# A seventh buffer for the scan's state tiles, with one buffer less in three other rings

## The chip, the cores and the metric

The kernel runs on one core of one Trainium2 chip. The metric is the device time of one execution in microseconds (us), as the median of several runs. A profile of one further execution is shown beside it. Engines are named as in the profile: PE is TensorE (PEld its weight loads), DVE is VectorE, ACT is ScalarE, POOL is GpSimd, SP is SyncE, which issues nearly all DMAs here; an engine's name with a q is its queue.

## The reference, cut to what matters

Two layers of a "metaformer" over an image batch `x` of 4 images of 64 x 64 positions and 128 channels. Layer 0 mixes with a four-direction state-space scan and then applies a soft mixture of 64 experts; layer 1 mixes rows and columns and then applies spectral filters (an FFT convolution). The change is in the scan of layer 0:

```python
x0 = xc.reshape(Bsz, DI, L)                       # DI = 256 channels, L = 4096 positions
x1 = jnp.transpose(xc, (0, 1, 3, 2)).reshape(Bsz, DI, L)
xs = jnp.stack([x0, x1, x0[..., ::-1], x1[..., ::-1]], axis=1)      # K = 4 directions
...
def step(h, xs):                                  # over L, per image, direction, channel, N = 16 states
    ut, dt, bt, ct = xs
    dA = jnp.exp(dt[..., None] * A)
    h = dA * h + (dt * ut)[..., None] * bt[:, :, None, :]
    y = jnp.einsum('bkdn,bkn->bkd', h, ct)
    return (h, y)
```

After it come the sum over the directions, a layer norm, a gate `z`, an output projection and the residual. All is float32.

## The kernel before, in words

**Scan part.** For each of 4 images and 4 directions the 4096 positions are cut into 8 chunks of 512. A chunk has 16 steps, one for each state index n; so there are 4 x 4 x 8 x 16 = 2048 steps s. Channels lie on partitions, in two halves of 128, and a step handles [128, 2, 512]:

- SP loads `bc` (L1460 to L1464): row n of B and of C for this chunk, spread over all partitions. Six buffers, asked for five steps ahead.
- ACT makes `da` = exp(delta x A_n), two activations (L1471). Five buffers, asked for three steps ahead.
- DVE makes `db` = (delta x u) times B into PSUM (L1501; the factor is `dx` in SBUF at n = 0 and its PSUM copy `du`, made by ACT at L1452, at the others), then runs two hardware scans h = da h + db along the 512 positions into `hh` (L1507).
- POOL keeps the last column for the next chunk (`hst`, L1516) and multiplies `hh` in place by C (L1517).
- PE transposes `hh` in eight 128 x 128 matmuls into the PSUM tile `y` (L1543), which adds up over the 16 steps. There is one `y`; at a chunk's end ACT copies it to `ys` (L1411, `put_away`), and only then may the next chunk's first transpose start.

`hh` is a ring of six tiles (L1497), 4 KiB per partition each. Scan s writes the tile that step s-6 used, so it waits until PE's transposes of step s-6 are done. The loop is skewed: its pass s traces scan s, POOL's work of s-1 and PE's of s-2. The next chunk's delta, `dl` and `dx` are made during the present chunk (`step_sizes`, L1342 to L1405: PE projection, ACT functions, POOL differences, PE sum).

**Side work.** All other stages are generators that yield weights. `deal` (L1420) runs after the first and after the second half of each step's transposes and takes as many pieces as are due, so that each image's share is used up evenly. What it traces is tied behind the step's instructions on each engine (`add_manual_dep`, "queued behind"), and later transposes on PE behind the side work. Within these ties the order of each engine's queue is laid down when the kernel is built, by readiness in the builder's own picture of time; so on ACT, for instance, a `da` that is traced later can stand ahead of a copy that is traced earlier. On the chip each queue keeps that order. During image 0 the side work is the front stages of the other images; during image b > 0 it is `after_scans`, `experts_and_sums`, `to_slots` of image b-1 and part of the spectral filters (`convolve`).

**Tail.** After the last scan the same stages for image 3 run (`first_stages`), woven with the remaining filters, then the return to positions (`from_slots`). The scan's tiles are gone then.

**The other rings.** `after_scans` works in 16 groups of 256 positions, as a pipeline whose later stages are traced first in each pass: load, `add` (evicts `y`, L534, ring of eight), norm sums, refine, a pause, `apply` (loads the gate `z`, L541 and L542, ring of five), a pause, `turn` (transposes of `y`, L552), the POOL product with `z` (L591), a pause, projection, store. `y` here is an SBUF tile of 2 KiB, apart from the scan's PSUM `y`; `z` is 2 KiB. `experts_and_sums` reads the first expert weights in 32 pairs through `w1t` tiles of 4 KiB (pool `ex1`, L822, ring of eight; loads at L835, asked for three pairs ahead; matmuls at L842). These stages run beside the scan and again in the tail.

Of the kernel before, what the change touches and what calls it, by code (L numbers as in the profile page):

```python
# [10 lines left out]
F32 = mybir.dt.float32  # L11
# [6 lines left out]
P = 128  # L18
B, H, W, C = 4, 64, 64, 128
L = H * W  # L20
DI, N, K, R = 256, 16, 4, 8
# [7 lines left out]
SC = 512  # L29
# [49 lines left out]
def kernel(  # L79
# [153 lines left out]
    def bank(shape, name):  # L233

        if side["ones"]:
            settle(1)
            return side["ones"].tile(shape, F32, name=name, tag="ps")
        n = int(np.prod(shape[1:]))
        ap = pair(name)[0 : shape[0], 0, 0:n]
        if len(shape) == 2:  # L240
            return ap
        sizes = {f"d{i}": d for i, d in enumerate(shape[1:])}
        names = " ".join(sizes)
        return ap.rearrange(f"p ({names}) -> p {names}", **sizes)
# [263 lines left out]
    def after_scans(b):  # L508

        with tc.tile_pool(name="po", bufs=2) as po:  # L510
            yk, y, z, xr, st, yT, pr = {}, {}, {}, {}, {}, {}, {}

            def rows(g):
                return slice(256 * g, 256 * (g + 1))

            def load(g):
                for k in range(K):
                    t = po.tile([P, 2, DI], F32, name=f"yk{k}")
                    yk[g, k] = t
                    if k % 2 == 0:  # L520
                        src = y_d[b][k, rows(g), :].rearrange("(q p) d -> p q d", p=P)
                        nc.sync.dma_start(t, src)
                    else:
                        byc = y_d[b][k].rearrange("(w q i) d -> i w q d", w=W, i=2)
                        for i in range(2):
                            nc.sync.dma_start(
                                t[i * W : (i + 1) * W], byc[i][:, 2 * g : 2 * g + 2]
                            )

            def add(g):  # L530
                ps = bank([P, 2, DI], "yk_ps")
                for k in range(K):
                    nc.tensor.matmul(ps, ident, yk.pop((g, k)), start=(k == 0), stop=(k == K - 1))  # L533
                y[g] = po.tile([P, 2, DI], F32, name="y", bufs=8)  # L534
                evict_soon(lambda: evict(y[g], ps))

            def sums(g):
                st[g] = norm_sums(po, y[g], 2, DI, eps5)

            def apply(g):  # L540
                z[g] = po.tile([P, 2, 256], F32, name="z", bufs=5)  # L541
                nc.sync.dma_start(z[g], z_d[b][:, :, rows(g)].rearrange("h p l -> p h l"))  # L542
                xr[g] = po.tile([P, 2, C], F32, name="xr", bufs=7)
                nc.sync.dma_start(xr[g], x[b, rows(g), :].rearrange("(q p) c -> p q c", p=P))
                norm_apply(y[g], y[g], st[g], 2)

            def turn(g):
                yT[g] = po.tile([P, 2, 256], F32, name="yT", bufs=4)
                ps = bank([P, 2, 2, P], "yt_ps")
                for h in range(2):  # L550
                    for q in range(2):
                        nc.tensor.transpose(  # L552
                            ps[:, h, q, :], y[g][:, q, h * P : (h + 1) * P], ident
                        )
                for h in range(2):
                    nc.scalar.activation(
                        yT[g][:, h, :],
                        ps[:, h].rearrange("p q t -> p (q t)"),
                        AF.Identity,
                        bias=nb[:, h : h + 1],  # L560
                        scale=nw[:, h : h + 1],
                    )

            def project(g):

                ps = bank([P, 2, C], "pr_ps")
                nc.tensor.matmul(ps, ident, xr[g], start=True, stop=False, skip_group_check=True)
                for q in range(2):
                    for h in range(2):
                        nc.tensor.matmul(  # L570
                            ps[:, q, :],
                            yT[g][:, h, q * P : (q + 1) * P],
                            w_out_t[:, h, :],
                            start=False,
                            stop=(q == 1 and h == 1),
                            skip_group_check=True,
                        )
                pr[g] = po.tile([P, 2, C], F32, name="pr", bufs=4)
                evict_soon(lambda: evict(pr[g], ps))

            yield from pipelined(
                16,
                (1.0, load),
                (2.2, add),
                (2.0, sums),
                (1.2, lambda g: norm_refine(po, st[g], 2, DI, 1e-5)),
                None,
                (1.2, apply),
                None,
                (1.0, turn),  # L590
                (1.2, lambda g: nc.gpsimd.tensor_mul(yT[g], yT[g], z[g])),  # L591
                None,
                (1.4, project),
                (
                    0.4,
                    lambda g: nc.sync.dma_start(
                        x1_d[b][rows(g), :].rearrange("(q p) c -> p q c", p=P), pr[g]
                    ),
                ),
            )  # L600
# [114 lines left out]
    def experts_and_sums(b):  # L715

        with tc.tile_pool(name="mk", bufs=1) as kp:
# [3 lines left out]
            with tc.tile_pool(name="ga", bufs=2) as gp:  # L721
# [70 lines left out]
                po = bank([P, E], "po_ps")  # L792
# [26 lines left out]

            EG = 2  # L820
            hT = kp.tile([P, HC, E], F32, name="hT")
            with tc.tile_pool(name="ex1", bufs=8) as ep:  # L822
                mask = ep.tile([P, 2, 32 * 32], F32, name="mask1", bufs=1)
                nc.gpsimd.memset(mask, 0.0)
                yield 2.0
                nc.gpsimd.tensor_copy(
                    mask[:, :, 0 : 32 * 32 : 33], pooled.rearrange("p (g e) -> p g e", g=2)
                )
                b1t = ep.tile([E, HID], F32, name="b1t", bufs=1)
                nc.sync.dma_start(b1t, w1[:, C, :])  # L830
                w1t = {}

                def load1(i):
                    w1t[i] = ep.tile([P, EG, HID], F32, name="w1t")
                    nc.sync.dma_start(  # L835
                        w1t[i], w1[i * EG : (i + 1) * EG, 0:C, :].rearrange("e d h -> d e h")
                    )

                def first(i):
                    for e in range(EG):  # L840
                        g, r = divmod(i * EG + e, 32)
                        nc.tensor.matmul(  # L842
                            hps[32 * g : 32 * g + 32, :],
                            mask[:, g, 32 * r : 32 * r + 32],
                            w1t[i][:, e, :],
                            start=(r == 0),
                            stop=(r == 31),
                            skip_group_check=True,
                        )

                for i in range(3):
                    load1(i)
                yield LAG
                hps = bank([E, HID], "h1_ps")
                for i in range(E // EG):
                    if i + 3 < E // EG:
                        load1(i + 3)
                    first(i)
                    yield 4.5
                h1 = ep.tile([E, HID], F32, name="h1", bufs=1)  # L860
                evict(h1, hps)
                yield LAG
                nc.gpsimd.tensor_add(h1, h1, b1t)
                yield LAG
                gelu = nc.scalar.activation(h1, h1, AF.Gelu)
                with tc.issue_after(gelu.ins):
                    nc.scalar.preload_act_table_set("natural_log_exp_and_others")
                yield LAG
                ps = bank([P, HC, E], "hT_ps")
                for q in range(HC):  # L870
                    nc.tensor.transpose(ps[:, q, :], h1[:, q : HID : HC], ident[0:E, 0:E])
                evict(hT, ps)
                yield LAG
            with tc.tile_pool(name="ex2", bufs=6) as ep:
# [31 lines left out]
                for i in range(E // EG):  # L906
                    if i * EG % 32 == 0:
                        g = i * EG // 32
# [421 lines left out]
    with ExitStack() as c0:  # L1330
        pb = c0.enter_context(tc.tile_pool(name="pb", bufs=2))
# [112 lines left out]
        bcs, das, hhs, dus, hsts, ys = {}, {}, {}, {}, {}, {}  # L1444
# [9 lines left out]
        for s in range(-5, total + 2):  # L1454
# [23 lines left out]
            if 0 <= s < total:  # L1478
# [12 lines left out]
                if i + 1 < len(chunks):  # L1491
# [2 lines left out]
                        sizes[i + 1] = step_sizes(nb_, nk, nci)  # L1494
                    if n >= 1:
                        next(sizes[i + 1][3], None)
                hhs[s] = pb.tile([P, 2, SC], F32, name="hh", bufs=6)  # L1497
                db = bps.tile([P, 2, SC], F32, name="db")

                src = sizes[i][1] if n == 0 else dus[i]  # L1500
# [25 lines left out]
            if n == 0:  # L1526
                y = ys[c] = bps.tile([P, 4, 2, P], F32, name="y")
# [165 lines left out]
```

## Time and profile before

| | |
|---|---|
| median of 3 runs | 10992.57 us (10983.71 to 10992.90) |
| the profiled execution | 10988.03 us, its span 10986.2 us |
| scan part, first `db` to the last step | 277 to 8797 us |
| tail | 8797 us to the end |
| busy, share of the span | PE 79%, DVE 75%, POOL 62%, ACT 57% |
| PE clock granted, scan part / tail | 0.83 / 0.99 |
| DMA | 1980 MB, 180 GB/s over the span |

A row of the costliest groups reads: line, engine, operation, written tile <- read tiles, shapes, count | busy us, mean ns of one | idle us of the engine just before them, and what ended most of it. In the slices each digit is the busy share of one fortieth of the span (275 us) in tenths. In the timeline the columns are start, duration, engine, line, operation and, in brackets, the idle time ahead of it with what ended it.

### The profile page before, as it was taken

How to read it: one execution, taken by the hardware profiler on the slowest of the kernel's cores; microseconds unless marked ns; L12 is line 12 of the kernel's file. 1: busy time of each engine (PE TensorE's matmuls, PEld its weight loads, DVE VectorE, ACT ScalarE, POOL GpSimd, SP SyncE). 2: the span in 40 equal slices, each digit the busy share in tenths (PEclk: the TensorE clock that was granted, in tenths of full speed). 3: DMA queues.
4: the chain of work that ended last, by engine and by line, in shares of the span. 5: the costliest groups of instructions: out<-in, count | busy, mean ns of one | idle time of the engine just before them, and what ended most of it. 6: DMA issues, size and time to landing. Idle time of an engine off the chain costs nothing. (4 is left out here: it accounts for less than half of the span.)

```text
span 10986.2 us, 119383 instructions
## 1 busy us (share of the span) xinstructions
PE 8713.2 (79%) x35936; PEld 4918.8 (45%) x35936; DVE 8219.8 (75%) x7094; ACT 6229.3 (57%) x12156; POOL 6822.5 (62%) x6102
## 2 busy tenths in 40 slices
PE   6787777657876777768777677687777799999999
PEld 2444444434454444455543344455344444355443
DVE  0898989987998999989989899798799922222322
ACT  4767676758576655675755557657556534134221
POOL 1777777977777888877777788677688811001000
PEclk9798888768888888878878888798788999999999
DMA  2465656657656666657566567475666564544554
GB/s 95 165 203 173 208 180 214 207 185 219 229 191 196 196 189 194 210 166 264 174 187 179 173 189 225 163 258 161 197 189 195 180 163 122 149 126 105 136 135 118
DMA packets 901464, 1980.28 MB, mean 180 GB/s; under 512 B 101562, under 2 KB 415578, under 8 KB 899290
## 3 DMA queue, kind: packets, MB, share of 16 engines
q1 hardware_dynamic: 900826, 1972.65, 58.8%
q8 instruction: 293, 4.80, 0.2%
q14 instruction: 345, 2.83, 0.1%
HBM read 1766.77 MB, written 205.52 MB: 180 GB/s over the span
## 5 line engine op out<-in xcount | busy, mean ns | idle before, releaser
L1517 POOL TENSOR_TENSOR hh<-hh,bc 128x1024 f32<-128x1024 f32 x2048 | 4876.0, 2382 | 424.6 <-DVE hh L1507 201.0
L1507 DVE TENSOR_TENSOR_SCAN hh<-da,hst,db 128x512 f32<-128x512 f32 x3584 | 4393.2, 1267 | 581.6 <-PE y L1543 186.7
L1471 ACT ACTIVATE da<-dl,aneg 128x512 f32<-128x512 f32 x4096 | 2768.6, 717 | 1889.1 <-DVE hh L1507 1814.9
L1543 PE MATMUL y<-ident,hh 128*128 128x128 f32 x16384 | 2643.7, 310 | 591.5 <-POOL hh L1517 512.8
L1543 PEld LDWEIGHTS y<-ident,hh 128*128 128x128 f32 x16384 | 2200.7, 160 | 1966.9 <-issue 1035.2
L1501 DVE TENSOR_TENSOR db<-du,bc 128x1024 f32<-128x1024 f32 x1920 | 2365.6, 1232 | 153.4 <-ACT du L1452 64.2
L1170 PE MATMUL cv_ps<-slab,us 64*128 64x512 f32 x4096 | 1165.7, 677 | 516.7 <-ACT y L257 287.3
L257 ACT COPY y<-cv_ps 128x512 f32<-128x512 f32 (+1 forms) x1024 | 754.9, 742 | 745.3 <-PE cv_ps L1170 709.9
L1516 POOL COPY hst<-hh 128x2 f32<-128x2 f32 x1792 | 392.0, 219 | 1090.9 <-DVE hh L1507 960.6
L1191 PE MATMUL zq_ps<-y,me 128*128 128x512 f32 x2048 | 995.3, 606 | 39.3 <-ACT y L257 37.5
L1191 PE MATMUL zq_ps<-y,mo 128*128 128x512 f32 x2048 | 980.9, 603 | 0.0
L1170 PEld LDWEIGHTS cv_ps<-slab,us 64*128 64x128 f32 x4096 | 398.2, 202 | 968.8 <-ACT y L257 373.6
L1207 POOL TENSOR_TENSOR zt<-zt,zt 128x512 f32<-128x512 f32 x64 | 81.1, 1267 | 1208.7 <-DVE zt L255 608.8
L255 DVE COPY y<-cv_ps 128x512 f32<-128x512 f32 x640 | 441.4, 691 | 508.3 <-PE cv_ps L1170 456.8
L1507 DVE TENSOR_TENSOR_SCAN hh<-da,db 128x512 f32<-128x512 f32 x512 | 596.8, 1207 | 60.8 <-PE y L1543 18.9
L411 PE MATMUL cv_ps<-xh,diag 128*128 128x512 f32 x1152 | 526.3, 599 | 10.3 <-ACT dl L1396 7.0
L1191 PEld LDWEIGHTS zq_ps<-y,me 128*128 128x128 f32 x2048 | 349.9, 192 | 368.8 <-issue 261.0
L1191 PEld LDWEIGHTS zq_ps<-y,mo 128*128 128x128 f32 x2048 | 361.0, 193 | 321.0 <-issue 319.0
L1361 PE MATMUL dt_ps<-dts,dtw 8*128 8x512 f32 x512 | 356.9, 811 | 141.4 <-ACT zt L257 43.1
L1501 DVE TENSOR_TENSOR db<-dx,bc 128x1024 f32<-128x1024 f32 x128 | 196.8, 1537 | 326.2 <-POOL dx L1403 318.0
L1387 POOL TENSOR_TENSOR ex<-ex,dx 128x1024 f32<-128x1024 f32 x128 | 302.3, 2362 | 160.6 <-ACT dx L1384 81.8
L255 DVE COPY zt<-zq_ps 128x512 f32<-128x512 f32 x42 | 29.0, 691 | 491.2 <-PE zq_ps L1191 486.8
(235 smaller groups left out, 9312.4 us busy)
## 6 DMA issues: line engine op xcount, KB each, us to landing
bc<-bc_d SPq DMA_DIRECT2D x2048, 512.0 KB
slab<-hd SPq DMA_DIRECT2D x1024, 256.0 KB
xc<-xc_d SPq DMA_DIRECT2D x128, 512.0 KB
y_d<-ys SPq DMA_DIRECT2D x128, 512.0 KB
w1t<-in_w_dram SPq DMA_DIRECT2D x128, 512.0 KB
w2t<-in_w_dram SPq DMA_DIRECT2D x256, 256.0 KB
xc_x<-xc_d SPq DMA_DIRECT2D x64, 512.0 KB
yk<-y_d SPq DMA_DIRECT2D x128, 256.0 KB
```

What stands on the lines that cost most here:

```text
L255: nc.vector.tensor_copy(dst, src)
L257: nc.scalar.copy(dst, src)
L411: nc.tensor.matmul(ps, diag[:, h, t, :], xh[:, 8 * g + dy : 8 * g + dy + 8, dx : dx + W], start=(t == 0), stop=(t == 8),)
L1170: nc.tensor.matmul(pq[q].rearrange("p (r k t) -> p r k t", r=2, t=BS), us[b, G][rows, p, a if e == 0 else 1 - a, :], slab[i][rows, p, :, : ...
L1191: nc.tensor.matmul(z, (me, mo)[e][:, KQ * kq + k, :], ys[e][:, :, :, :, k, :].rearrange("p a q r t -> p (a q r) t"), start=(e == 0 and k = ...
L1361: nc.tensor.matmul(ps, dtw[:, k, h * P : (h + 1) * P], dts, start=True, stop=True)
L1471: i_act = nc.scalar.activation(das[t][:, h, :], sizes[t // N][0][:, h, :], AF.Exp, scale=aneg[:, tk, h, t % N : t % N + 1],)
L1501: nc.vector.tensor_mul(db, src, bcs[s][:, 0:1, :].to_broadcast([P, 2, SC]))
L1507: i_dve = nc.vector.tensor_tensor_scan(o, d0, d1, init, ALU.mult, ALU.add)
L1516: nc.gpsimd.tensor_copy(hsts[t // N][:, :, t % N], hhs[t][:, :, last])
L1517: i_pool = nc.gpsimd.tensor_mul(hhs[t], hhs[t], bcs.pop(t)[:, 1:2, :].to_broadcast([P, 2, SC]))
L1543: i_pe = nc.tensor.matmul(ys[c][:, q, h, :], hhs[t][:, h, q * P : (q + 1) * P], ident, is_transpose=True, start=(n == 0 and k > 0 and q % ...
```

## The change

The ring of `hh` gets a seventh tile (4 KiB more per partition during the whole scan part). `after_scans` loses one `y` and one `z` (2 + 2 KiB), and the `ex1` pool one `w1t` (4 KiB). No instruction is added or taken away.

```diff
-                y[g] = po.tile([P, 2, DI], F32, name="y", bufs=8)
+                y[g] = po.tile([P, 2, DI], F32, name="y", bufs=7)
...
-                z[g] = po.tile([P, 2, 256], F32, name="z", bufs=5)
+                z[g] = po.tile([P, 2, 256], F32, name="z", bufs=4)
...
-            with tc.tile_pool(name="ex1", bufs=8) as ep:
+            with tc.tile_pool(name="ex1", bufs=7) as ep:
...
-                hhs[s] = pb.tile([P, 2, SC], F32, name="hh", bufs=6)
+                hhs[s] = pb.tile([P, 2, SC], F32, name="hh", bufs=7)
```

## The prediction, made before the result was known

> **What bounds the kernel now.** I read the page first: busy time by slice, then the costliest groups.
>
> ```profile
> PE   6787777657876777768777677687777799999999
> DVE  0898989987998999989989899798799922222322
> POOL 1777777977777888877777788677688811001000
> ...
> L1517 POOL TENSOR_TENSOR hh<-hh,bc 128x1024 f32<-128x1024 f32 x2048 | 4876.0, 2382 | 424.6 <-DVE hh L1507 201.0
> L1507 DVE TENSOR_TENSOR_SCAN hh<-da,hst,db 128x512 f32<-128x512 f32 x3584 | 4393.2, 1267 | 581.6 <-PE y L1543 186.7
> ```
>
> There are two regimes. Up to slice 32 DVE is 80 to 90% busy and nobody else is; in the last eight PE is at 90% or more and DVE at 20%. The stretches view gives the split: from 277 us (first db product) to 8797 us (last scan step) DVE is busy 7637 of 8520 us; from there to the end PE is busy 2130 of 2189 us. So the scan part is DVE's, the tail PE's, and only the first has hh in it.
>
> One step of DVE is a product (1.23 us), a gap of 0.13, two scans (2.45 together) and a gap of 0.04: 3.85 us, from the median rows of the timeline. 2048 of these are 7885 us; the part takes 8520. The 635 us between are what any buffer can be worth at most. Who holds them, from the view of the scan's line:
>
> ```profile
> its engine sat idle before it (us, times) until:
>   PE y L1543: 205.6, 79
>   ACT da L1471: 92.7, 31
>   ACT y L257: 25.8, 7
> ```
>
> Scan s writes the hh tile that PE's eight transposes of step s-6 must have read. The first line is this wait. This view names the releaser that came last by its semaphores; pairing the records step by step (k-th scan, k-th group of eight L1543 matmuls) I find 104 scans that start within 0.6 us of the end of y(s-6) and later than the usual 0.13 us after their db: 277 us in all. The usual distance from that end to the scan is 0.20 us. So PE's lag through the ring is the largest single loss, 2.5% of the span, and the rest (late da 124 us, late dx and du 131 us at the first two steps of a chunk, small gaps) does not depend on the ring.
>
> **How a ring wait comes about.** The timeline at a chunk's end shows one kind:
>
> ```profile
> 3029.32 1.33 ACT L1471 ACTIVATE da<-dl,aneg 128x512 f32<-128x512 f32 x2 [2.52 <-DVE hh L1507]
> ...
> 3030.56 1.05 ACT L1411 COPY ys<-y 128x512 f32<-128x512 f32 x2
> ...
> 3031.71 1.09 PE L1543 MATMUL y<-ident,hh 128*128 128x128 f32 x4 [9.68 <-ACT ys L1411]
> ...
> 3036.05 1.28 DVE L1507 TENSOR_TENSOR_SCAN hh<-da,hst,db 128x512 f32<-128x512 f32 x1 [1.65 <-PE y L1543]
> ```
>
> PE had finished the chunk at 3022.0, but ACT's copies that free the y tile stand behind a da activation, and that waits for a scan. PE gets y back 9.7 us late, and five steps on DVE waits 1.65 us. Walking each of the 104 waits back through PE and its releasers, 35 (82 us) end like this, at a da that waited for scan s-3 or later. The other 69 (195 us) end at a load, a GpSimd piece or older PE work: the largest burst, 67 us between 7668 and 7800, hangs on round trips through DRAM (ub, ud, zb, slab).
>
> **What the Trainium skill says.** "Perfetto Trace Analysis", Optimization Strategy: find the gaps of the contended engine and the semaphore that ends them; a gap that repeats can mean that there is not enough SBUF for the next tile (buffer count). The trace agrees on which wait, but it doesn't repeat evenly: 104 of 2048 steps, in 52 bursts. Same page, Sequencer Loop: instructions are pushed into an engine's queue and wait there for their semaphores. The trace shows the order holding: ys waited behind da. "SBUF — State Buffer", SBUF size: about 208 KiB per partition are usable on trn2, which is why a tile has to be given up elsewhere; no run so far shows the limit.
>
> **The change part by part.**
>
> *hh from six to seven.* No instruction is added or removed. Scan s now waits for y(s-7). Cost nothing; gain bounded per burst: with PE's clock times fixed, the seventh tile lets DVE go one step further, so a burst gives back min(burst, 3.85) once. The 52 bursts are 19 under 1.5 us, 18 up to 3.85, 10 up to 10, 5 above; the sum of the minima is 123 us. Bursts with several separate PE delays can give more than once (each wait capped singly: 199), and a second burst soon after a first gives less, since DVE comes to it early while PE does not. So I ran down the list as a recurrence over the trace's own times: a scan starts at the later of (its old start, less its ring wait, less the gain so far) and (the old end of y(s-7) + 0.20, less the gain that PE has had passed on). The one free choice is how many steps later PE gets a gain: at once 146 us, after 7 steps 116, after 16 98, after 32 70.
>
> The 35 waits behind a da need a second look, since ACT's order is laid down when the kernel is built and may move with the ring. da(t) can run when scan t-5 is done. In ACT's order the ys copies of a chunk ending at step e stand behind da(e+5) to da(e+10): 16, 8, 22, 36, 27 and 18 of 127 times. e+10 is as far as six tiles allow, since scan e+6 is the first that needs y(e). With seven, these 18 can slip to e+11; then y comes back a step later, DVE waits a step later, and nothing is won. If the 35 waits stay as they are, the recurrence gives 108, 90, 75 and 59. I take this case, with PE following 7 to 16 steps later (PE is 75% busy in this part, so it catches up within about a chunk): mean of 90 and 75, **82 us**.
>
> What is late next: DVE then meets da, dx and du, which come through ACT and GpSimd from DVE's own earlier steps; they move with it and are counted at their present size.
>
> *y of the output stage from eight to seven.* y(g) is evicted at the pipeline step after its load and last read by the transposes six steps later. From the records, the eviction of y(g) starts at least 14.8 us after the transposes of g-7 ended, in all four images. So a ring of seven would not have held one of them: 0. The cover is one pipeline step; gone, the eviction would wait on ACT with da behind it.
>
> *z from five to four.* The load of z(g) waits for the GpSimd product of g-4 instead of g-5. Against present times 4 of the 36 loads that a ring of four would gate in the first three images (12 each) come too early, by 0.8, 0.8, 3.3 and 1.1 us: 6 us of waiting on SP's queue in the kernel. Behind such a load stand SP's bc loads, for which DVE would wait. These are issued five steps ahead, about 19 us of cover, and DVE's present waits on bc are 18 us in all. I take 2 us, bounds 0 and 6. In the tail the least distance is 13.4 us: 0.
>
> *Expert weights, first layer, eight to seven.* Loads are asked for three pairs ahead. In the scan part the least distance from the seventh-last pair's matmuls to a load is 2.5 us: 0. In the tail SP runs as far ahead as the ring lets it (a load goes out 0.03 us after the eighth-last pair is done), some 7 us per pair. With seven it goes out a pair later but still some 49 us ahead of use: 0, hidden by the filter matmuls that keep PE busy. A slab load queued behind it could be up to 7 us later; slabs go two parts ahead, and a part takes about 14 us (160 parts in 2189 us). If that cover failed, PE would pay up to 7 us once, as every later load is shifted alike.
>
> *Sum:* 82 - 2 = **80 us**. The profiled execution took 10988.03 us (span 10986.2, 1.8 around it); it would become 10908. It lies 4.5 below the median of 10992.57 and inside the runs, so for the median I say 10992.6 - 80 = **10912**.
>
> **Rivals.** (1) *The full ring gain*: ACT's order stays, and the 35 waits shrink too: 116 to 146 us, **10862**. For it: most chunk ends (109 of 127) stand below the limit of the order. Against: the waits in question belong to the other 18 and their like. (2) *The order cancels it*: queues on ACT and GpSimd follow the ring one step everywhere, so PE's lag grows by the step that the ring gained; within 22 us of now, **10985**. For it: ACT waited 1815 us for scans before da, in 962 steps, so whatever stands behind da is late already. Against: 195 of the 277 us come from loads and PE work that da doesn't delay. (3) *A new wait at the chunk's start, slower*: du. DVE's second step needs the ACT copy of dx into PSUM; hh has no part in that. The copy ends less than 3.85 us before use in 53 of 127 chunks, dx in 10. If deeper running ahead sets these behind one more da or side activation, each costs 3.85 less its present distance: 122 us for du and 31 for dx, 153 at most. Once over half of that comes true it eats the gain of 80; at three quarters the time is 10992.6 + 115 - 80 = **11028**. Against it: da and du are both driven by DVE's own progress, which the ring doesn't reorder.
>
> **Chances.** Forecast (gain 22 to 116) 0.54; (1) 0.12; (2) 0.16; (3) 0.18. About 0.2%, 22 us, is what a measurement of this kernel can tell from no change. Faster 0.66, same 0.16, slower 0.18. The range runs from the top of (1), 146 us and a little, 10840, to 11010, inside (3); it leaves out some 0.16, nearly all above. The forecast's own range is 10876 to 10970.
>
> **What would show it.** In the profile after: the scan's wait on PE y falls from 205.6 to about 130 us or less; DVE's busy share up to slice 32 rises by 1%; the tail keeps its 2189 us; da waits stay near 93; SP's wait for z stays under 10 us. If scans wait for du or dx by tens of us more, (3) holds. If PE y stays near 200 with the ys copies behind da(e+11), (2) does. A tail longer by over 20 us would make the ring cuts wrong.

## The result and the profile after

| | before | after |
|---|---|---|
| median of 5 runs | 10992.57 us (10983.71 to 10993.0) | 10936.89 us (10933.26 to 10938.76) |
| the profiled execution | 10988.03, span 10986.2 | 10933.26, span 10931.4 |
| scan part, first `db` to the last scan's end | 8502.8 us | 8446.7 us |
| tail | 2189.2 us | 2189.4 us |

The ratio is 0.9952 (95% interval 0.9941 to 0.9963): 56 us faster, where 80 were forecast, and inside the range. All of it lies in the scan part. (The first `db` starts at 294.2 us. The 277 us given ahead lie 17 us earlier, so the part lasted 8502.8 us before, not 8520.)

From the page of the changed kernel, two rows of slices and the group of the scans:

```profile
PE   6787777657786777768777777787777799999999
...
DVE  0888989988998999989989899798899922222322
...
L1507 DVE TENSOR_TENSOR_SCAN hh<-da,hst,db 128x512 f32<-128x512 f32 x3584 | 4392.8, 1266 | 487.8 <-PE y L1543 134.6
```

The two regimes stand as before. The idle time ahead of the scans is down by 94 us (581.6 to 487.8), and PE is still its largest releaser, with 134.6 in place of 186.7. The scan part of the changed kernel, again counted from 277 us, with length, busy time of PE, PEld, DVE, ACT and POOL, granted clock, DMA share and GB/s:

```profile
277.00:8743.00 8466.00, 6320.02 (x28324) 3841.56 (x28322) 7650.65 (x6240) 5453.02 (x10281) 6624.62 (x5629) 0.84 0.62 197
```

DVE's share is 90.4%, against 89.6% before (7637 of 8520). But its busy time also grew, from 7637 to 7651 us, though it does the same work: some of DVE's instructions take longer (see the last section). The view of the scan's line, after:

```profile
its engine sat idle before it (us, times) until:
  PE y L1543: 143.4, 52
  ACT da L1471: 89.7, 29
```

The wait on the ring fell from 205.6 to 143.4 by this view. Paired step by step as in the prediction (scan s against the end of y(s-7)) it fell from 277 us in 104 scans to 163 in 56: by 114. Since the kernel gained 56, half was given back. The view of the product's line shows where; first before, then after:

```profile
  POOL dx L1403: 318.0, 9
  ACT du L1452: 64.2, 17
  DMA bc<-bc_d: 18.3, 5
```

```profile
  POOL dx L1403: 319.6, 9
  ACT du L1452: 76.9, 23
  DMA bc<-bc_d: 34.3, 12
```

(284 us of the first line is the one start of the scan part.) By pairing every step of DVE with its operands, us and, in brackets, times. The third column is experiment 2 below, seven tiles with the queues laid out as for six:

| DVE in the scan part | before | after | seven tiles, laid out for six |
|---|---|---|---|
| first scan of a step waits for the ring | 277.1 (104) | 163.3 (56) | 110.9 (36) |
| first scan waits for `da` | 91.9 (30) | 78.8 (30) | 81.8 (28) |
| second scan waits for `da` | 33.4 (8) | 48.9 (9) | 28.9 (8) |
| product waits for `du` | 63.6 (17) | 76.1 (23) | 84.8 (24) |
| product waits for `bc` | 18.1 (5) | 33.9 (12) | 31.6 (12) |
| product at n = 0 beyond its usual 1.23 us | 38.6 (30) | 52.5 (38) | 51.2 (34) |
| first `db` to last scan | 8502.8 | 8446.7 | 8393.9 |

Before to after that is 114 + 13 won, 12.5 + 15.8 + 13.9 + 15.5 = 58 given back, and some 13 more in rows that are not listed (4 of them at `dx`) and in short gaps: 56.

### The profile page after: what moved, and what is told of

It is laid out like the page before. It is cut to its first block, busy times and chain, and to the rows that moved or that the text cites. A ratio compares the mean times of both kernels' runs of the same rounds, so it can differ in the third digit from the quotient of the medians.

```text
span 10931.4 us, 119319 instructions
## 1 busy us (share of the span) xinstructions
PE 8642.8 (79%) x35936; PEld 4876.0 (45%) x35936; DVE 8233.2 (75%) x7094; ACT 6232.6 (57%) x12156; POOL 6817.4 (62%) x6102
## 5 line engine op out<-in xcount | busy, mean ns | idle before, releaser
L1507 DVE TENSOR_TENSOR_SCAN hh<-da,hst,db 128x512 f32<-128x512 f32 x3584 | 4392.8, 1266 | 487.8 <-PE y L1543 134.6
L1543 PE MATMUL y<-ident,hh 128*128 128x128 f32 x16384 | 2605.4, 307 | 552.8 <-POOL hh L1517 474.7
L1543 PEld LDWEIGHTS y<-ident,hh 128*128 128x128 f32 x16384 | 2169.9, 159 | 1914.6 <-issue 1012.9
L1191 PE MATMUL zq_ps<-y,me 128*128 128x512 f32 x2048 | 998.4, 608 | 38.6 <-ACT y L257 35.3
```

The lines of the kernel that those rows point to most:

```text
L1191: nc.tensor.matmul(z, (me, mo)[e][:, KQ * kq + k, :], ys[e][:, :, :, :, k, :].rearrange("p a q r t -> p (a q r) t"), start=(e == 0 and k = ...
L1507: i_dve = nc.vector.tensor_tensor_scan(o, d0, d1, init, ALU.mult, ALU.add)
L1543: i_pe = nc.tensor.matmul(ys[c][:, q, h, :], hhs[t][:, h, q * P : (q + 1) * P], ident, is_transpose=True, start=(n == 0 and k > 0 and q % ...
```

## The experiments

Times are medians. Each ratio is to the kernel before as measured in the same batch: 10987.35 us for experiments 1 to 4, 10995.30 for 5 to 8, 10999.56 for 9 to 12. Times of different batches are better compared by their ratios.

**1. The cuts alone.** The changed kernel with `hh` back at six.

```diff
-                hhs[s] = pb.tile([P, 2, SC], F32, name="hh", bufs=7)
+                hhs[s] = pb.tile([P, 2, SC], F32, name="hh", bufs=6)
```

> hh stays at six; only y, z and w1t lose their tile. Theory (the cut rings are free, all of the change is the hh ring): within 0.1% of the kernel before, 10993 +- 12 us, and the scan's wait on PE y stays at 206 us. Rival (the cuts cost time and hid a part of the gain, since 56 us came instead of 80): some 24 us slower than before, about 11017, with SP waits at the z load or a longer tail.

Measured: 10985.79 us, ratio 1.0000 (0.9992 to 1.0008). The scan's line:

```profile
  PE y L1543: 207.0, 74
```

The three smaller rings cost nothing that can be measured, and they do not touch the ring wait (205.6 before).

**2. Seven tiles, queues laid out as for six.** The order of each queue is laid down by the builder, in whose picture scan s may run as soon as its tile is free. A tie (an ordering edge for the builder; nothing waits for it on the chip) makes it believe that scan s still needs PE's transposes of step s-6. I call the 6 the layout's lead. On six tiles the ring itself asks for these transposes, so six is the lead that the builder has by itself there. With seven tiles the tie brings most of that order back, though not item for item: of the 10256 instructions on ACT in the scan part 299 stand at another place than in the kernel before, against 1298 without the tie. The line that ties (`y_last[t]` is the name of the last transpose of step t):

```diff
-                    i_dve = nc.vector.tensor_tensor_scan(o, d0, d1, init, ALU.mult, ALU.add)
+                    i_dve = nc.vector.tensor_tensor_scan(o, d0, d1, init, ALU.mult, ALU.add); s - 6 in y_last and tc.add_manual_dep(i_dve.ins, y_last[s - 6], order, reason="as with six")
```

> hh has seven tiles as in the changed kernel, but an ordering edge (no wait on the chip) from scan s to PE's transposes of step s-6 makes the builder lay out the queues as for six tiles. Theory A (the queues on ACT and POOL moved one step with the ring and ate a part of the gain, at the ring and at du, bc and the first products): 10900 to 10915 us, 80 to 90 us faster than before; the scans' ring wait falls below the 163 us of the changed kernel to about 130, and the wait on du returns to 64. Rival B (the order is of no matter; DVE comes earlier and then meets da, du and bc, whatever their order): 10937 +- 10 us, the same as the changed kernel, with the ring wait at about 163 and the other waits as large as there.

Measured: 10881.50 us (10880.23 to 10883.67), ratio 0.9904 (0.9891 to 0.9918). The scan's line and the product's:

```profile
  ACT da L1471: 96.0, 34
  PE y L1543: 71.3, 29
```

```profile
  ACT du L1452: 85.7, 24
  DMA bc<-bc_d: 32.0, 12
```

With the queues nearly as before the tile is worth 106 us, and some 55 of them are lost when the queues follow the ring (10936.9 against 10881.5; 53 by the ratios). That is more than theory A expected, and the ring wait, 110.9 us by pairing, is below its 130. But one part of the theory failed: the wait on `du` did not go back to 64, it is 84.8. So the return through `du` is not made by the new order. One way in which they follow is the position of `ys` on ACT. In the changed kernel 11 of 127 chunk ends have it behind da(e+11), where six tiles allowed e+10 at most; with the tie none has. Such an end in the timeline of the changed kernel (e = 95):

```profile
696.41 1.33 ACT L1471 ACTIVATE da<-dl,aneg 128x512 f32<-128x512 f32 x2 [1.59 <-DVE hh L1507]
...
698.22 1.06 ACT L1411 COPY ys<-y 128x512 f32<-128x512 f32 x2
...
699.33 3.66 PE L1531 MATMUL y<-skip,xc 128*128 128x128 f32 x16 [6.38 <-ACT ys L1411]
...
704.07 2.45 DVE L1507 TENSOR_TENSOR_SCAN hh<-da,hst,db 128x512 f32<-128x512 f32 x2 [2.58 <-PE y L1543]
```

The scan at n = 7 waits 2.58 us. In the kernel before, the scan at n = 6 of this chunk waited 2.60 us (it started at 700.27), and the two steps after it not at all. The extra tile let one more step through, and `ys` came one `da`, and so one step, later: nothing won at this chunk. With the tie (experiment 2) the same chunk end reads

```profile
685.90 1.06 ACT L1411 COPY ys<-y 128x512 f32<-128x512 f32 x2
687.01 3.78 PE L1531 MATMUL y<-skip,xc 128*128 128x128 f32 x16 [4.60 <-ACT ys L1411]
...
689.30 2.45 DVE L1507 TENSOR_TENSOR_SCAN hh<-da,hst,db 128x512 f32<-128x512 f32 x2
...
693.16 2.45 DVE L1507 TENSOR_TENSOR_SCAN hh<-da,hst,db 128x512 f32<-128x512 f32 x2
```

and neither n = 6 (689.30) nor n = 7 (693.16) waits.

**3. Only the `ys` copies held back to their old limit.** In the changed kernel, da(e+8) is tied behind ys(e) (`ys_last` holds the name of each chunk's last `ys` copy):

```diff
-                    )
+                    ); t % N == 7 and 0 < t // N <= len(ys_last) and tc.add_manual_dep(i_act.ins, list(ys_last.values())[t // N - 1], order, reason="behind ys")
```

> The changed kernel, with an ordering edge that puts da(e+8) behind the ys copies of the chunk that ends at step e, so that no ys copy stands behind more than da(e+7). Theory A (order of ACT's queue makes the chunk-end ring waits): the waits of scans 4 to 8 of a chunk, 51 us in the changed kernel, fall to under 20, and the time is 10900 to 10915 us. Rival B (these waits turn into waits for da, which now stands behind ys): da waits rise by 20 us or more and the time stays at 10937 +- 10.

Measured: 10914.83 us, ratio 0.9932 (0.9918 to 0.9946). The scan's line:

```profile
  PE y L1543: 111.2, 32
  ACT da L1471: 111.0, 44
```

Against the changed kernel this gains 22 us, where experiment 2 gains 55. Pairing finds the ring wait down to 140.8, with the waits of the scans n = 4 to 8 down from 51.5 only to 38.6, not below 20 as expected, and the wait for `da` up from 78.8 to 101.2: a `da` now has to stand behind the copy. The time just reaches theory A's range, and the waits for `da` are what rival B expected. So `ys` is a part of what the layout does, and not the whole.

**8. Both at once**: seven tiles, the tie of six and the tie of `ys`.

> Seven tiles, the cut rings, the edge to step s-6 and the edge that puts da(e+8) behind the ys copies. Theory A (both take away waits behind da, partly the same ones): 10865 to 10880 us. Rival B (the ys edge moves waits from the ring to da, as it did with 22 us on its own): 10881 us or slower.

Measured: 10886.34 us, ratio 0.9900 (0.9885 to 0.9914), against 0.9904 without the `ys` tie: what the rival expected. Once the layout is that of six, `ys` has nothing more to give.

**4. Five tiles**, to see the same term with the other sign: the kernel before with one less.

```diff
-                hhs[s] = pb.tile([P, 2, SC], F32, name="hh", bufs=6)
+                hhs[s] = pb.tile([P, 2, SC], F32, name="hh", bufs=5)
```

> The kernel before, with five hh tiles and nothing else changed. Theory (a ring wait is a queue between two engines that are both nearly full, each tile less costs more than the last): the recurrence run the other way gives 184 to 340 us lost for fixed queues; if the queues move with the ring and give back a part as they took one, 80 to 180 us: 11070 to 11170 us, and the scan's wait on PE y grows to 330 us or more. Rival (the ring mattered at a few DMA round trips only, which cost one step each): some 50 us, 11045.

Measured: 11110.08 us, ratio 1.0112 (1.0098 to 1.0125). The scan's line:

```profile
  PE y L1543: 317.4, 119
```

The time fell inside what was expected; the ring wait is just below the 330 that I had set. The rows that grew with the seventh tile shrink with the fifth taken away (product waits for `du` 33.9 in 8, for `bc` 4.3 in 2): they are the other end of the same time. By pairing, the ring wait grew by 227 us (277 to 505) and the time by 123: about half was met by other waits that became shorter.

**5 and 6. A lead one less, on six and on seven tiles.** If the builder's lead and the ring's depth are two things, six tiles laid out for five should gain too, with no memory at all. Same edit with s-5, on the kernel before and on the changed one. In the scan part the two traces show the same order on every engine, so what differs is the tile and the three cut rings, which experiment 1 found free.

> The kernel before (six hh tiles, all other rings as before) with the ordering edge from scan s to PE's transposes of step s-5: the queues are laid out as for five tiles, the chip has six. Theory A (it is the builder's order at the full ring that makes a part of the ring waits): the ring wait falls from 277 us to about 210, and the time to 10930 to 10955 us without any new tile. Rival B (the edge helps only together with the seventh tile, or it delays da and POOL's products so that DVE waits for those): 10987 +- 10 us or slower, with da waits up by 20 us or more.

> Seven tiles and the cut rings, with the same edge to step s-5: in the scan part every queue is the same as in the six-tile kernel with this edge, so the pair measures the seventh tile alone. Theory A: the recurrence for fixed queues gives 98 to 146 us less ring wait, of which some 45 us come back as waits for du, bc and the first products: 60 to 100 us faster than its six-tile pair, and 10850 to 10890 us. Rival B (these next waits take most of the tile's worth): under 40 us faster than the pair.

Measured: 10881.07 us, ratio 0.9893 (0.9878 to 0.9908), better than expected, and 10837.99 us, ratio 0.9852 (0.9836 to 0.9869). The scan's line of the first, then of the second:

```profile
  PE y L1543: 90.8, 34
```

```profile
  PE y L1543: 55.4, 18
```

Two readings. Six tiles with the tie reach the time that seven reach with the layout of six: 10881.1 and 10881.5 (0.9893 and 0.9904). And the tile by itself, the queues being the same, is worth 43 us by the medians, short of the 60 to 100 that theory A expected and just above the 40 of its rival. By pairing, the ring wait falls by 76 (165.8 to 89.9), and `du` (51.8 to 77.4), `bc` (15.0 to 33.8) and `da` (93.7 to 100.1) give 51 back. The ring wait fell by less than the 98 to 146 expected, as those had been taken from the kernel before. (The two profiled executions, to which these waits belong, differ by 28 us, 10874.53 and 10846.73, which would be the rival's case; the medians by 43.) The 51 us are the return without any change of order.

**7. Seven tiles, a lead of four.**

> Seven tiles, the cut rings, and the edge to step s-4. Theory A (the further the laid-out lead stays below the ring, the fewer waits stand behind da; returns get smaller): 10850 to 10885 us, ring wait under 90. Rival B (a lead of four is too short: loads, da and POOL's products are laid out later than DVE needs them): over 10900 us, with waits for da or bc up by 30 us.

Measured: 10831.27 us, ratio 0.9851 (0.9836 to 0.9866); the scan's wait on PE y is 47.4, the product's on `du` 81.4. Level with a lead of five (0.9852), and better than expected.

**9 and 10. Is it the layout or the distance between lead and depth?** Five and six tiles, both laid out for four. Their traces and that of experiment 7 show the same order on every engine in the scan part.

> Five hh tiles, all other rings as before, the edge to step s-4: every queue the same as with six and seven tiles and this edge, up to the tail. Theory S (what counts is how many tiles the ring has beyond the lead that the queues were laid out for, here one): like the other kernels with one tile beyond, 10881 us, within 20; so over 90 us faster than six tiles laid out for six. Rival R (the number of tiles itself counts, and the layout is a smaller second effect): 10950 us or more.

> Six tiles, all other rings as before, the edge to step s-4; two tiles beyond the layout, and no memory given up. Theory S: 10840 +- 12 us, as seven tiles laid out for five (10838), and within 20 us of seven laid out for four (10831). Rival R: a tile is worth its 43 us here too, so 10874 us or more.

Measured: 10940.23 us, ratio 0.9947 (0.9935 to 0.9960), and 10850.71 us, ratio 0.9865 (0.9850 to 0.9880). With five, the scan's line:

```profile
  PE y L1543: 194.4, 69
```

Had only the distance of one counted, five laid out for four would stand with the pairs of experiments 2 and 5, at 10881; it doesn't. Nor does it come to the 10950 or more that the rival asked for. Six laid out for four came to the upper edge of what theory S expected. Both count: the lead moves the time, and so does each tile, less with each one. The product's line for six tiles (experiment 10) and then seven (experiment 7), with the queues the same:

```profile
  ACT du L1452: 45.5, 15
```

```profile
  ACT du L1452: 81.4, 24
```

**12. A lead of three on seven tiles.**

> Seven tiles, the cut rings, the edge to step s-3, one nearer than before. Theory S with returns getting smaller: 10825 to 10840 us, ring wait under 80. Rival (a lead of three starts to hold back da, bc and POOL's products in the queues): over 10850 us, with waits for da or bc up by 20 us or more.

Measured: 10860.33 us, ratio 0.9876 (0.9862 to 0.9889). The scan's line, then the product's:

```profile
  PE y L1543: 39.8, 11
```

```profile
  ACT du L1452: 132.0, 30
  DMA bc<-bc_d: 53.2, 31
```

Too short a lead: the ring wait is the smallest of all, and `du` the largest, 50 us above its 81 at a lead of four. The time is as the rival expected, but the wait that grew is this one; `bc` grew by 10 (43.0 to 53.2) and `da` not at all.

**11. The tile given to `bc` instead.** The changed kernel's cuts, `hh` six, `bc` seven, a lead of four.

```diff
-                bcs[t] = pb.tile([P, 2, SC], F32, name="bc", bufs=6)
+                bcs[t] = pb.tile([P, 2, SC], F32, name="bc", bufs=7)
```

> The same with the memory that the change gave up (y 7, z 4, w1t 7) used for a seventh bc tile instead of a seventh hh tile. Theory (after the ring, DVE meets loads of bc that SP issues late because their tile comes free late): the wait on bc falls from some 35 us to under 10, and the time by 15 to 30 us against its pair without it. Rival (SP is late because of what else stands in its queue, not because of the tile): no change, within 10 us.

Measured: 10814.76 us (10806.93 to 10816.01), ratio 0.9832 (0.9819 to 0.9846), the fastest of all: 36 us less than with `bc` at six (experiment 10). But the reason that I gave is not shown: that pair's wait for `bc` was 9.0 us, so it could not give 36. The scan's line:

```profile
  PE y L1543: 77.6, 26
```

The ring wait by pairing fell by 31 us (168.2 to 136.7), and the queues of ACT and SP are in another order than the pair's. Whether the earlier loads, that order or the rings cut for it did it stays open.

**All of them by tiles and lead** (ratio to the kernel before; "own" is the layout that the builder makes by itself):

| tiles | own (lead = tiles) | six | five | four | three |
|---|---|---|---|---|---|
| five | 1.0112 | | | 0.9947 | |
| six | 1 | (own) | 0.9893 | 0.9865 | |
| seven | 0.9952 | 0.9904 | 0.9852 | 0.9851 | 0.9876 |

Read down the column of four: the sixth tile is worth 90 us (10940 to 10851), and the seventh 15 to 20 (by ratio or median, from two batches, with intervals that overlap). Read along seven: 10937, 10881, 10838, 10831, 10860. No run has eight tiles.

## Why the prediction was right and where it was off

**The seventh tile.** Mechanism and sign were right: the largest single loss of DVE was PE's lag through the ring, and a tile takes part of it. The ring term was taken at 82 us; measured by the same pairing it was 114, close to the 116 of the full recurrence with PE following seven steps later. The nearness to 116 is partly luck, for the recurrence takes the queues as fixed, and they moved: with nearly the old order (experiment 2) the ring wait fell by 166, more than the 146 of PE following at once. The same recurrence on pairs whose queues are the same, with PE following at once and then 16 steps later, gives 71 to 58 us for experiments 5 and 6, where 76 were measured, 65 to 49 for 10 and 7 (83 measured) and 185 to 140 for 9 and 10 (150 measured). So it sizes the ring wait fairly to a little low. The waits by scan show DVE coming one step further: the largest was at n = 13 with 56 us before, and is at n = 14 with 38 after.

Three readings of the prediction were off without changing its sum. POOL stands at 80% or more in 10 of the first 32 slices, so "nobody else" is too strong. The 635 us hold 17 us ahead of the first `db` and 95 us of DVE's own side work, which no buffer of the scan gives back. And late `dx` and `du` are 98 us by the view of the product's line (318.0 - 284.2 + 64.2), not 131.

**The step that failed is "What is late next":** `da`, `dx` and `du` "move with it and are counted at their present size". They did not keep it. Some 58 us came back in four rows of the table above, a term that the sum had at nothing. With the ring at 114 the account closes: 114 + 13 - 58 - 13 is 56. The assumption failed because it saw DVE's operands as driven by DVE alone. `du` is a copy on ACT, and ACT's queue also carries evictions that wait for PE. The timeline of the changed kernel shows it:

```profile
5704.92 0.66 PE L1213 MATMUL zt_ps<-ident,zt 128*128 128x128 f32 x4 [1.14 <-ACT y L257]
...
5705.62 0.59 ACT L257 COPY zo<-zt_ps 128x512 f32<-128x512 f32 x1 [0.75 <-PE zt_ps L1213]
...
5707.34 1.21 ACT L1452 COPY du<-dx 128x512 f32<-128x512 f32 x2
...
5708.58 1.23 DVE L1501 TENSOR_TENSOR db<-du,bc 128x1024 f32<-128x1024 f32 x1 [1.59 <-ACT du L1452]
```

`du` stands behind `zo`, an eviction of a spectral filter that waits for PE, and behind a `da`; DVE then waits 1.59 us. The chunks 80 to 85 have this wait each, 1.1 to 1.8 us; before, three of the six had one. So PE's lag has several doors to DVE, and a tile closes a part of one. The kernels with the same queues show it. Each `du` wait is walked back along ACT's queue to the last instruction that had stood idle for over 0.1 us in the 12 us ahead of the copy, and is put down to what that one waited for (us, by pairing):

| tiles, lead | ring wait | `du` wait, put down to PE | `du` wait, all else |
|---|---|---|---|
| five, four (experiment 9) | 318 | 8.0 | 24.6 |
| six, four (10) | 168 | 19.2 | 25.7 |
| seven, four (7) | 85 | 44.1 | 36.3 |
| six, five (5) | 166 | 20.0 | 31.8 |
| seven, five (6) | 90 | 44.6 | 32.8 |

As the ring wait falls, it is the part put down to PE that grows most; the part put down to POOL stays at 16 to 17 in all five. In experiment 12 the part put down to PE is 92.7 of 131 us. From before to after it rose from 24.9 to 37.3, nearly all of the 12.5 at `du`. The loads of `bc` stand on SP's queue behind stores of `uo` and `ht` (L1111, L705), and these wait for ACT's evictions of PE's results: such a store stood in the 6.5 us ahead of the late load for 11.6 us of the `bc` waits before and for 23.5 after. The other two rows are of another kind. All that second scans lost more at `da` lies in four steps in a row (1612 to 1615), and first scans won 13 at `da`; the 13.9 at the first products belong to the last section. The Trainium skill, "Perfetto Trace Analysis", section Sequencer Loop, says that an instruction pushed into an engine's queue waits there for its semaphores; the lines above show it once more, and show that what stands behind it waits too (`du` behind `zo`).

**Rival (2), that the order cancels it,** was half of the truth and was given too little room beside the forecast. Its mechanism is real: the builder moved 11 chunk ends to e+11, and with the layout held at six the same tile gives 106 us. It took some 55 us, not all. I had argued against it that 195 of the 277 us end at loads and PE work that `da` does not delay. That held for `ys`, which is a smaller part (experiment 3: holding it alone brings 22 of the 55), and missed the rest of the layout. Which other items of ACT's, SP's or PE's queues make the remaining 33 was not separated.

**Rival (3), du as a new wait,** was right in kind and wrong in size: 12.5 us, where 153 was its ceiling. **Rival (1)** came near the ring term with its 116, and left out what comes back.

**The smaller rings.** `y` at seven and `w1t` at seven: 0 as predicted. `z` at four: the records of the changed kernel show the four held loads that were forecast, on SP's queue,

```profile
SPq L542 <- POOL hst L1516: 6.7, 4, 3.5
```

6.7 us in four, against 6 in four. The 2 us taken for DVE's part cannot be told from zero (experiment 1: within 0.08% of no change, so under 9 us either way). The tail kept its 2189 us.

**What was to be seen.** PE y "to about 130 or less": 143. `da` near 93: 90 for the first scans, though the second scans gained 15. SP's wait on `z` under 10: 6.7. DVE's share up by 1 point: 0.8, a part of it only longer instructions. The gain was 30% below the forecast.

## What to carry to other kernels

Where queue orders are laid down at build time from the builder's own picture of time, the depth of a ring does two things: it gives slack on the chip, and it tells the builder how far ahead it may place work. Set them apart: lay the queues out for one or two buffers fewer than there are, with an edge that orders the build and waits for nothing. Here that gave 114 us at six buffers laid out for five, with no memory, and 149 laid out for two fewer, where the seventh buffer gave from some 20 (not clear of the intervals) to 106 by the layout it came to and, with the layout following, 56; too short a lead gives it back. And when a wait on a lagging engine is to be bought off with a buffer, list every other queue through which the same lag reaches the bound engine, and count what comes through them as growing. With the queues the same, a buffer cut the ring wait by 150, 76 and 83 us here, and the time by 90, 43 and some 20.

## What the runs showed of the hardware that was not expected

The busy time that DVE gained is in the products at n = 0, which read two tiles in SBUF (`dx` and `bc`); with `du`, which is in PSUM, the product took 1.203 to 1.241 us in every profile, 1920 times each. At n = 0 its median is 1.24 us, its longest 3.38 in the kernel before, 10.49 in the changed one and 12.80 in experiment 2. The longest one of the changed kernel:

```profile
7741.65 2.79 POOL L1289 TENSOR_TENSOR xr<-xr,iv 64x256 f32<-64x256 f32 x4
7742.36 10.49 DVE L1501 TENSOR_TENSOR db<-dx,bc 128x1024 f32<-128x1024 f32 x1
...
7744.40 4.63 POOL L1517 TENSOR_TENSOR hh<-hh,bc 128x1024 f32<-128x1024 f32 x2
...
7748.99 2.76 POOL L1289 TENSOR_TENSOR xr<-xr,iv 64x256 f32<-64x256 f32 x4
```

POOL ran without a gap from 7741.65 to 7751.75, and the product ended 1.10 us after that, at 7752.85: about its own length. The Trainium skill, "SBUF — State Buffer", section "SBUF: two separate sides", describes such a thing: DVE and GpSimd share a pair of ports under an exclusive lock, which a DVE operation with two SBUF inputs and a GpSimd operation that reads SBUF contend for, and the one that starts second is blocked. It says for the whole of the other's instruction; here it lasted through some nine POOL instructions in a row. The records of all fourteen profiles fit it: 492 first products took over 1.295 us, and every one of them ended 1.085 to 1.097 us after the end of a POOL instruction. The products with `du` began over 0.2 us before a POOL instruction's end some 600 to 800 times in each profile, and none took over 1.241 us. So the wait goes with the operand in SBUF and with POOL's work; that it is this lock is read from the skill's description, and no run isolates it. All first products together lose 38.6 us in 30 before and 52.5 in 38 after; why they meet POOL's work more often with the seventh tile was not tried.
